# Conditional pairs for the routed blocks that may be empty, and four reorderings in the later stages of a fused kernel

## The chip, the cores and the metric

The kernel runs on one core of a Trainium2 chip. The time is the device time of one execution in microseconds (us), and the median of three runs is what counts: 2526.67 us before the change. A core has five engines that work side by side, each through its own list of instructions: TensorE (PE; its weight loads are listed as PEld), VectorE (DVE), ScalarE (ACT), GpSimd (POOL) and SyncE (SP). Data move by DMA, started from an engine's queue. All of the program is one launch.

## The reference

There are 32 sequences of 128 rows, N = 4096 rows, each with D = 512 channels. Four blocks follow each other, with a residual after the second and after the fourth:

```
# 1: shared expert plus two of eight routed experts per row
shared = (silu(x @ sw1.T) * (x @ sw3.T)) @ sw2.T
e1, e2 = top_k(sigmoid(x @ router.T + t_bias) + router_bias, 2)
out = (shared + sum_e gate_e * (gelu(x @ rw1[e].T) @ rw2[e].T)) / 3
# 2: per sequence, a policy picks one of eight weight sets
sel = argmax(policy(out[:, -1]))
x1 = x + out + 0.3 * ((gelu(out @ W1[sel] + b1[sel]) @ W2[sel] + b2[sel]) @ Wo + bo)
# 3: mix with the row before, sixteen experts by token id with a capacity
xk, xr = x1 + dx * maa_k, x1 + dx * maa_r      # dx = previous row - row
y = sigmoid(xr @ w_recept) * expert_out[slot]  # square(relu(xk @ w_key[e])) @ w_value[e]
# 4: recurrence over the 32 sequences with forget, input and candidate gates
c = sigmoid(y @ wf + c @ uf + bf) * c + sigmoid(y @ wi + c @ ui + bi) * tanh(y @ wc + c @ uc + bc)
h = tanh(y @ wo + c_final @ uo + bo); result = x1 + h
```

What each row is routed to is known only while the kernel runs.

## The kernel before

Products are made in three matmuls (`mm3`, L81): `split` (L63, L64) makes a high part on ACT (a cast to fp32r) and a low part on DVE (a subtract). Transposes are matmuls against `ident`. Tile pools hand out buffers by tag; an instruction waits until the last reader of the buffer is done. The order of instructions on each engine follows the program, but `tc.issue_after(x)` and `behind(pair)` (L71) place an instruction after x in the planned order.

The stages, with their times in the profiled execution:

- **Shared expert and router, 0 to 307 us.** The first four of eight row groups go through the shared expert. `choose` (L456) counts the rows of each expert, and pads each expert's list to blocks of 128 rows. `blk_t` holds the row numbers of a block, `blk_e` the column of its expert's weights, `end` (L496) the block at which each expert ends.
- **Routed blocks, 307 to 557 us.** At worst 71 blocks are needed (`NBLK`, 64 full ones and 7 for padding), and all 71 are always run by the loop at L689. In iteration i PE does `r_up(i)` (L658: a register load of blk_e on PE, twelve matmuls 128x256 into pur), `turn_x(i + 1)` (L283: four transposes into ptx, and a split), then `r_down(i - 1)` (L681: six matmuls 128x512 into por, a copy on DVE, a 256 KB store on SP) and `turn_h(i)` (L672: two transposes into pth, and a split). `take(i + 3)` (L275) gathers rows by an indirect DMA on POOL's queue. Blocks past the last used one hold only padding.
- **Shared expert again, 557 to 842 us.** The other four groups, with the routed rows added. In the last group `hook2` (L939) fetches the first three weight sets of the next stage and splits them with `split_w` (L878) at its chunks c = 5, 6 and 7; each split releases the gather of the weight set three further on (`fetch_w`, L859, three raw buffers).
- **Stage B, 842 to 1457 us.** A loop over the sequences (L1177) interleaves `up`, `bend` (transposes, gelu, split), `down`, each in halves a and b. `turn_r` (L1069) transposes ps and adds the bias in eight operations, four on ACT and four on DVE, into rT. Every two sequences `close` (L1086) makes x1 and xk, `mix_r` (L1134) makes xr, `send_k` (L1148, tile ptB) stores rows of xk, and `send_v` (L1158, tile pv) those of v. The weight split of a sequence is skipped when the policy picked the same set as for the one before: a branch on ACT and DVE (L891). `used` calls `split_w` after each use of a weight half.
- **Stage D, 1457 to 1834 us.** The sixteen experts. Their rows are gathered from `xk_d` once the stores of the last two `send_k` are done (rowsD, tile ptD).
- **Stage F, 1834 us to the end.** The recurrence. Its weights wc, wi and wf are fetched on ACT's queue from L1533 and uf on SP's (L1528), through a pool `stage` that is opened and closed there; rows y are gathered on POOL's queue (`get_y`, L1406) and gated (`gate_y`, L1423, tile ptF).

```
            for i in range(NBLK + 1):
                if i < NBLK:
                    r_up(i)
                    turn_x(i + 1, bx, "xb")
                    take(i + 3)
                if i > 0:
                    stored = r_down(i - 1)
                if i < NBLK:
                    turn_h(i)
```

Of the kernel before, what the change touches and what calls it, by code (L numbers as in the profile page):

```python
# [8 lines left out]
F32 = mybir.dt.float32  # L9
# [28 lines left out]
NBLK = (2 * N + E0 * (P - 1)) // P  # L38
EPS = 1e-9
# [9 lines left out]
def tile_kernel(ctx: ExitStack, tc: tile.TileContext, a: dict, out: bass.AP):  # L49
# [86 lines left out]
    blk_e = const.tile([P, NBLK], I32, name="blk_e")  # L136
    hl = const.tile([P, KD, NB], F32, name="hl")
# [10 lines left out]
    pad = const.tile([P, 448 // 4], F32, name="pad")  # L148
# [7 lines left out]
    with ExitStack() as sa:  # L156
# [117 lines left out]
        with ExitStack() as s0:  # L274
            def take(i):  # L275
                if i < NBLK:
                    xg[i] = xgp.tile([P, D], F32, tag="xg", name=f"xg_{i}")
# [5 lines left out]
            def turn_x(i, pool, tag, bufs=2):  # L283
                if i < NBLK:
# [4 lines left out]
                    if tag == "act":  # L289
# [166 lines left out]
            def choose():  # L456
# [40 lines left out]
                nc.vector.tensor_tensor(end, first, nblk, ALU.add)  # L497
                base = rtile([P, E0], "base")
# [152 lines left out]
        with s1:  # L651
# [6 lines left out]
            def r_up(i):  # L658
                with tc.issue_after(last_up[0]) if last_up else nullcontext():
                    e = nc.tensor.value_load(  # L660
                        blk_e[0:1, i : i + 1], min_val=0, max_val=(E0 - 1) * RCOL
                    )
# [9 lines left out]
            def turn_h(i):  # L672
# [4 lines left out]
                h = bx.tile([P, 2, HR // P, P], FR, tag="hb", name=f"hbr_{i}")  # L677
# [11 lines left out]
            for i in range(NBLK + 1):  # L689
                if i < NBLK:  # L690
                    r_up(i)
                    turn_x(i + 1, bx, "xb")
                    take(i + 3)
                if i > 0:
                    stored = r_down(i - 1)
                if i < NBLK:
                    turn_h(i)
                if i == NBLK - 16:
                    with tc.issue_after(stored):
                        fetch_x(NG // 2)  # L700
                if i == NBLK - 10:
# [173 lines left out]
        def bias_of(kind, b, o):  # L875
            return bcol[b][:, BIAS[kind] * KD + o : BIAS[kind] * KD + o + 1]
# [21 lines left out]
        with ExitStack() as s2:  # L898
# [40 lines left out]
            def hook2(g, c):  # L939
                sums(g, c)  # L940
                if g == last:
# [4 lines left out]
                    if c >= KF - AHEAD:  # L946
                        with behind(act_split):
                            split_w(c - KF + AHEAD)
# [15 lines left out]
    with ExitStack() as sb:  # L964
# [37 lines left out]
        def seq(p):  # L1002

            if p not in seqs:
                seqs[p] = nc.sync.value_load(seq_i[0:1, p : p + 1], min_val=0, max_val=PARTS[where(p)[0]] - 1)
            return seqs[p]

        def rows_of(t, p):

            return t[bass.ds((seq(p) + where(p)[0] * PARTS[0]) * P, P), :]  # L1010
# [58 lines left out]
        def turn_r(b):  # L1069
# [7 lines left out]
            for o in range(KD):  # L1077
                hi = rTs[c][:, 0, o, bass.ts(j, P)]
# [648 lines left out]
```

## Time and profile before

| what | value |
|---|---|
| three runs | 2520.85, 2526.67, 2529.47 us |
| profiled execution, its time | 2522.89 us |
| profiled execution, its span | 2521.2 us |
| mean granted clock of TensorE | 0.989 |
| matmuls | 13044 |
| routed blocks, 307.6 to 557.0 | 249.4 us, PE busy 247.3 |
| last matmul of the recurrence | near 2499 us |

The profile is of one execution. A page gives the busy time of each engine; the waits name, for each idle stretch of an engine, the instruction that ended it; windows give the busy times, the granted clock of TensorE and the share of the DMA engines for a stretch of time. The row of the granted clock, in 40 slices, with tenths of full speed, reads 9 almost throughout, which hides short stretches at half clock; these are seen in windows. A line number such as L660 is the kernel's, and names such as pt_0a are tiles of the program. Where several edits touch different stages, each stage is read on its own.

### The profile page before, as it was taken

What the parts mean: (1) busy time and instruction counts of PE and PEld (TensorE: products, weight loads), DVE (VectorE), ACT (ScalarE), POOL (GpSimd) and SP (SyncE); (2) the same over time, 40 slices, a digit from 0 to 9 for tenths busy, and PEclk for the clock granted to TensorE, in tenths of its full rate; (3) what the DMA queues carried; (4) which work ended last, traced back from release to release, by engine and by line L of the source; (5) the groups of instructions that cost most, each with busy time, mean ns of one, the idle gap of its engine ahead of it and who ended that gap; (6) DMA issues with size and microseconds to landing.
All of it is one profiled execution on the core that took longest, in us unless ns stands there. A gap on an engine that the chain in (4) does not pass through costs nothing. (4 is left out here: it accounts for less than half of the span.)

```text
span 2521.2 us, 37055 instructions
## 1 busy us (share of the span) xinstructions
PE 2455.6 (97%) x13044; PEld 2074.9 (82%) x13044; DVE 1331.5 (53%) x2341; ACT 1064.6 (42%) x1935; POOL 429.6 (17%) x460
## 2 busy tenths in 40 slices
PE   8999999999999899999999999999999999999996
PEld 5688899987888788888887889999978888888885
DVE  7797644556567444444454477667643323333336
ACT  4444533343223555455455466666532212222224
POOL 1000022222233333323223010000010000000003
PEclk9999999999999999999999999999999999999998
DMA  5545544457565333342342387776441111111027
GB/s 180 165 125 168 180 151 154 156 184 249 176 217 168 113 107 127 116 134 70 104 146 96 123 295 226 231 234 224 139 160 42 38 38 38 43 42 42 25 80 267
DMA packets 193117, 351.11 MB, mean 139 GB/s; under 512 B 37473, under 2 KB 72337, under 8 KB 189857
## 3 DMA queue, kind: packets, MB, share of 16 engines
q1 hardware_dynamic: 141504, 244.42, 29.6%
q0 software_dynamic: 36160, 74.90, 10.3%
q10 hardware_dynamic: 15264, 29.37, 3.2%
q8 instruction: 108, 1.77, 0.3%
q14 instruction: 81, 0.66, 0.1%
HBM read 373.94 MB, written 88.13 MB: 183 GB/s over the span
## 5 line engine op out<-in xcount | busy, mean ns | idle before, releaser
L64 DVE TENSOR_TENSOR wD<-rawD,wD 128x1024 fp32r<-128x1024 f32 x128 | 156.4, 1229 | 77.4 <-ACT wD L63 77.2
L81 PE MATMUL p<-xhl,swu 128*128 128x512 f32 x768 | 188.0, 396 | 5.5 <-ACT xhl L63 5.5
L81 PEld LDWEIGHTS phD<-xe,wD 128*128 128x128 f32 x1536 | 184.6, 189 | 1.2
L81 PE MATMUL phD<-xe,wD 128*128 128x256 f32 x1536 | 185.3, 281 | 0.0
L81 PE MATMUL p<-xhl,kept_u 128*128 128x512 f32 x768 | 184.3, 394 | 0.7 <-DVE kept_u L64 0.7
L81 PE MATMUL poD<-wD,hD 128*128 128x512 f32 x768 | 181.3, 392 | 0.0
L81 PEld LDWEIGHTS p<-xhl,swu 128*128 128x128 f32 x768 | 143.8, 189 | 36.0 <-ACT xhl L63 5.8
L81 PEld LDWEIGHTS p<-xhl,kept_u 128*128 128x128 f32 x768 | 141.8, 188 | 30.1 <-DVE kept_u L64 1.1
L81 PEld LDWEIGHTS poD<-wD,hD 128*128 128x128 f32 x768 | 142.0, 188 | 28.4
L63 ACT CAST wD<-rawD 128x1024 fp32r<-128x1024 f32 x128 | 133.1, 1046 | 53.4 <-PE poD L81 48.7
L278 POOL DMA_INDIRECT xg<-in_x_rows_dram,blk_t x71 | 67.6, 952 | 463.4 <-PE ptx L288 257.8
L1409 POOL DMA_INDIRECT y<-res_d,gat_i x32 | 33.3, 1040 | 573.9 <-DVE r L1428 495.2
L81 PE MATMUL pur<-r,xb 128*128 x852 | 118.2, 288 | 0.7 <-DVE xb L64 0.4
L81 PE MATMUL por<-r,hbr 128*128 x426 | 116.3, 407 | 1.4 <-ACT hbr L63 1.3
L64 DVE TENSOR_TENSOR xb<-ptx,xb 128x512 fp32r<-128x512 f32 x71 | 49.1, 692 | 115.3 <-ACT xb L63 115.3
L81 PEld LDWEIGHTS pur<-r,xb 128*128 128x128 f32 x852 | 105.2, 189 | 1.7 <-ACT xb L63 0.7
L81 PE MATMUL ps_f<-wf_hl,z 128*128 128x512 f32 x384 | 96.5, 399 | 0.0
L81 PE MATMUL poF<-z,wo_hl 128*128 128x512 f32 x384 | 96.4, 399 | 0.0
L81 PE MATMUL acc<-swd,as 128*128 128x512 f32 x384 | 96.0, 395 | 0.0
L81 PE MATMUL ps_c<-wc_hl,z 128*128 128x512 f32 x384 | 95.1, 395 | 0.7 <-ACT z L63 0.7
L81 PE MATMUL pb<-rT,Wo_hl 128*128 128x256 f32 x768 | 94.6, 281 | 0.0
L81 PE MATMUL pv<-w_recept_hl,xr 128*128 128x512 f32 x384 | 94.3, 395 | 0.0
(1014 smaller groups left out, 5038.3 us busy)
## 6 DMA issues: line engine op xcount, KB each, us to landing
rawD<-in_w_key_dram SPq DMA_DIRECT2D x64, 512.0 KB, 4.1
rawD<-in_w_value_dram SPq DMA_DIRECT2D x64, 512.0 KB, 3.8
swr<-in_sw_dram SPq DMA_DIRECT2D x120, 256.0 KB, 3.7
o_d<-obr SPq DMA_DIRECT2D x71, 256.0 KB, 2.4
xraw<-in_x_dram SPq DMA_DIRECT2D x32, 256.0 KB, 3.8
rraw<-in_rw_dram SPq DMA_DIRECT2D x32, 256.0 KB, 3.4
xc<-in_x_dram SPq DMA_DIRECT2D x32, 256.0 KB, 3.5
hid_d<-o ACTq DMA_DIRECT2D x32, 256.0 KB, 2.2
```

The lines of the kernel that those rows point to most:

```text
L63: first = nc.scalar.copy(hi, src).ins
L64: done = nc.vector.tensor_tensor(lo, src, hi.bitcast(F32), ALU.subtract).ins
L81: done = nc.tensor.matmul(ps, lhsT=left(hl, k), rhs=right(hr, k), start=start and k + n == 0, stop=stop and 3 * k + n == last,)
L278: nc.gpsimd.indirect_dma_start(out=xg[i], out_offset=None, in_=a["x_rows"], in_offset=bass.IndirectOffsetOnAxis(ap=blk_t[:, i : i + 1], ax ...
L1409: nc.gpsimd.indirect_dma_start(out=y, out_offset=None, in_=res_d, in_offset=bass.IndirectOffsetOnAxis(ap=gat_i[:, b : b + 1], axis=0),)
```

## The change

It has a part in each of the later stages.

1. **Routed blocks.** Blocks 0 to 63 stay unconditional. Blocks 64 to 70 form the pairs (64,65), (66,67), (68,69) and (70). Each pair runs in a conditional (`maybe`) on PE, ACT, DVE and SP that compares `used_i`, the count of blocks in use, with the pair's first block. The four conditionals stand at iterations 16, 22, 28 and 34 of the loop. The body of a pair also transposes the rows of the next pair; those of the first pair are transposed in iterations 10 and 11. The gathers of all pairs run whether or not they are used, in iterations 6, 12, 18 and 24, and each gathered tile is also stored to its block's rows of `o_d` on SP's queue; a block that runs overwrites them. On the way that is not taken, each engine waits for its own earlier instructions and then raises its semaphores.
2. **Last shared group.** The three `split_w` calls move from chunks 5, 6, 7 to 4, 5, 6.
3. **Stage B.** `turn_r` becomes one addition of the bias on DVE, written back into ps, and one split. `send_v` of a pair moves to the next iteration, one of the two between `up(a)` and `turn_r` and the other after `down(a)`. `mix_r` moves from the end of `close` to the next iteration, behind the last split.
4. **End of stage B.** The last two `send_k` store on ACT's queue, with a register load on ACT, and what follows is ordered after the store's DMA.
5. **Start of stage F.** The weights are staged in the pool `zop`, which is opened first. wc, uf and wi are fetched on SP's queue before the first gates, wf on POOL's after the first gathers of y. Products with wc and wi come before that with wf, wo is fetched after the first two tiles of y are split, and three later loads wait for a later step.

The core of the diff:

```diff
+NFULL = 2 * N // P
...
-                    xg[i] = xgp.tile([P, D], F32, tag="xg", name=f"xg_{i}")
+                    pool, tag = (xgp, "xg") if i < NFULL else (bx, "xgm")
+                    xg[i] = pool.tile([P, D], F32, tag=tag, name=f"xg_{i}")
...
+                nc.vector.tensor_copy(used_i, end[:, E0 - 1 :])
...
-            def r_up(i):
-                with tc.issue_after(last_up[0]) if last_up else nullcontext():
-                    e = nc.tensor.value_load(
-                        blk_e[0:1, i : i + 1], min_val=0, max_val=(E0 - 1) * RCOL
-                    )
+            def first_col(i):
+                return nc.tensor.value_load(blk_e[0:1, i : i + 1], min_val=0, max_val=(E0 - 1) * RCOL)
+            def r_up(i, e=None):
+                if e is None:
+                    with tc.issue_after(last_up[0]) if last_up else nullcontext():
+                        e = first_col(i)
...
+            pairs = [range(i, min(i + 2, NBLK)) for i in range(NFULL, NBLK, 2)] + [range(0)]
+            FIRST, STEP = 16, 6
+            def maybe(n):
+                es = [first_col(i) for i in pairs[n]]
+                with tc.If(used > pairs[n][0]):
+                    for i, e in zip(pairs[n], es):
+                        r_up(i, e)
+                    for m in range(2):
+                        for i in pairs[n][m : m + 1]:
+                            turn_h(i)
+                        for i in pairs[n + 1][m : m + 1]:
+                            turn_x(i, xh, "x", KD)
+                    for i in pairs[n]:
+                        r_down(i)
+                last_up.clear()
+            for i in range(NFULL + 1):
+                if i < NFULL:
                     r_up(i)
-                    turn_x(i + 1, bx, "xb")
-                    take(i + 3)
+                    if i + 1 < NFULL:
+                        turn_x(i + 1, bx, "xb")
+                    if i + 3 < NFULL:
+                        take(i + 3)
                 if i > 0:
                     stored = r_down(i - 1)
-                if i < NBLK:
+                if i < NFULL:
                     turn_h(i)
-                if i == NBLK - 16:
+                n, step = divmod(i - FIRST, STEP)
+                if i == FIRST - 4:
+                    engines = (nc.tensor, nc.scalar, nc.vector, nc.sync)
+                    used = nc.values_load(
+                        used_i[0:1, 0:1], engines=[x.engine for x in engines], min_val=NFULL, max_val=NBLK
+                    )
+                if FIRST - 6 <= i < FIRST - 4:
+                    turn_x(pairs[0][i - FIRST + 6], xh, "x", KD)
+                m, ahead = divmod(i - FIRST + STEP + 4, STEP)
+                if ahead == 0 and 0 <= m < len(pairs):
+                    for q in pairs[m]:
+                        take(q)
+                        nc.sync.dma_start(out=o_d[q * P : (q + 1) * P, :], in_=xg[q])
+                if step == 0 and 0 <= n < len(pairs) - 1:
+                    maybe(n)
...
-                    if c >= KF - AHEAD:
+                    if 4 <= c < 4 + AHEAD:
                         with behind(act_split):
-                            split_w(c - KF + AHEAD)
+                            split_w(c - 4)
...
-            for o in range(KD):
-                hi = rTs[c][:, 0, o, bass.ts(j, P)]
-                done_a = nc.scalar.activation(hi, pt[:, o, :], AF.Identity, bias=bias_of("W2a", b, o))
-                done_v = nc.vector.scalar_tensor_tensor(
-                    rTs[c][:, 1, o, bass.ts(j, P)], pt[:, o, :], bias_of("W2a", b, o),
-                    hi.bitcast(F32), ALU.add, ALU.subtract,
-                )
-            return done_a.ins, done_v.ins
+            rT = ps.rearrange("p (k q) -> p k q", k=KD)
+            bias = bias_of("W2a", b, 0, KD).unsqueeze(2).to_broadcast([P, KD, P])
+            nc.vector.tensor_tensor(rT, pt, bias, ALU.add)
+            s = bass.ts(j, P)
+            split(rTs[c][:, 0, :, s], rTs[c][:, 1, :, s], rT)
+            return tuple(last_split)
...
-            done = nc.scalar.copy(rows, pt.rearrange("p k q -> p (k q)"))
-            nc.sync.dma_start(out=rows_of(xk_d, b), in_=rows)
-            return done.ins
+            nc.scalar.copy(rows, pt.rearrange("p k q -> p (k q)"))
+            return queue.dma_start(out=rows_of(xk_d, b, queue), in_=rows).ins
...
+            gated = b - 4 if b % 2 == 0 and 0 <= b - 4 < NB - 6 else None
+            if gated is not None:
+                send_v(gated)
             if 0 <= b - 1 < NB:
                 r_done = turn_r(b - 1)
             if 0 <= b < NB:
                 down(b, "a")
                 used()
+            if gated is not None:
+                send_v(gated + 1)
...
+            if j == 0 and 0 < c < NB // PB:
+                with behind(last_split) if b + 1 < NB else nullcontext():
+                    mix_r(c - 1, end_p if c == NB // PB - 1 else bp, "xr")
...
-            if pair is not None and pair < NB - 6:
-                send_v(pair)
             if b + 1 < NB:
                 bend(b + 1, "b")
-            if pair is not None and pair < NB - 6:
-                send_v(pair + 1)
...
-                if c < NB // PB - 2:
-                    mix_r(c, bp, "xr")
-                elif c == NB // PB - 2:
-                    mix_r(c, end_p, "xr")
...
-            rows_done = send_k(b)
+            rows_done = send_k(b, nc.scalar)
...
+        zop = sf.enter_context(tc.tile_pool(name="zop", bufs=4, side="right", **kw))
...
-        with tc.tile_pool(name="stage", bufs=4, side="right", **kw) as stage:
-            uc["f"] = weight("uf", uf_p, stage, 4)
-            for b in range(LEAD):
-                nc.scalar.activation(ys[b][1], ys[b][1], AF.Sigmoid)
-            for n in "cif":
-                from_c(0, n, ps, cT, True, False)
-            wx["c"] = weight("wc", wx_p, stage, 4, queue=nc.scalar)
-            with tc.issue_after(first_part["wc"]):
-                gate_y(0)
-                gate_y(1)
-            for b in range(LEAD):
-                get_y(b + LEAD)
-            for n in "if":
-                wx[n] = weight("w" + n, wx_p, stage, 4, queue=nc.scalar)
-        zop = sf.enter_context(tc.tile_pool(name="zop", bufs=1, **kw))
+        wx_hl = {n: wx_p.tile([P, 2, KD * D], FR, tag="w" + n, name=f"w{n}_hl") for n in "ifc"}
+        wx["c"] = weight("wc", wx_p, zop, 4, pair=wx_hl["c"])
+        uc["f"] = weight("uf", uf_p, zop, 4)
+        wx["i"] = weight("wi", wx_p, zop, 4, pair=wx_hl["i"])
+        for b in range(LEAD):
+            nc.scalar.activation(ys[b][1], ys[b][1], AF.Sigmoid)
+        for n in "cif":
+            from_c(0, n, ps, cT, True, False)
+        gate_y(0)
+        z_done = gate_y(1)
+        with tc.issue_after(first_got):
+            wx["f"] = weight("wf", wx_p, zop, 4, pair=wx_hl["f"], queue=nc.gpsimd)
+        for b in range(LEAD):
+            get_y(b + LEAD)
...
-                from_x(0, ps, "cif", False, True)
-                wo1 = weight("wo", keep_p, yp, 2, "zo", KD)
+                done = from_x(0, ps, "ci", False, True)
+                with tc.issue_after(done):
+                    from_x(0, ps, "f", False, True)
+                with tc.issue_after(z_done):
+                    wo1 = weight("wo", keep_p, yp, 2, "zo", KD)
...
-                load_part(first_p, "c0", "x", 3, 0)
-                load_part(first_p, "cT0", "x", 3, 1, 2)
+                with tc.issue_after(late):
+                    load_part(first_p, "c0", "x", 3, 0)
+                    load_part(first_p, "cT0", "x", 3, 1, 2)
```

## The prediction

> **What bounds the kernel now.** I read the page's busy shares first, then TensorE's (PE's) waits, then busy time and clock stage by stage.
>
> ```profile
> PE 2455.6 (97%) x13044; PEld 2074.9 (82%) x13044; DVE 1331.5 (53%) x2341; ACT 1064.6 (42%) x1935; POOL 429.6 (17%) x460
> ```
>
> ```profile
> 307.60:557.00 249.40, 247.31 (x1701) 223.57 (x1700) 124.15 (x215) 98.79 (x221) 63.28 (x67) 1.00 0.49 161
> 842.00:1457.50 615.50, 597.36 (x3208) 504.74 (x3208) 283.45 (x543) 315.21 (x701) 180.43 (x178) 0.98 0.36 115
> ...
> 1834.20:1870.00 35.80, 31.45 (x132) 24.57 (x131) 20.76 (x26) 18.50 (x25) 10.43 (x9) 0.90 0.69 227
> ```
>
> PE is busy 97% of the span: only fewer matmuls, fewer PE gaps or a higher clock can shorten it. The rows are stretches: start and end, length, then PE, PEld, DVE, ACT and POOL busy, granted clock, DMA share. The routed blocks (first row) have almost no gap; stage B (second) loses 18 us to gaps and some to the clock; the start of the recurrence (third) is the worst in proportion.
>
> ```profile
> PE pt_0a L1050 <- ACT ue_0a L1043: 7.0, 1, 7.0
> ...
> PE ptD L1304 <- DMA rowsD<-xk_d,slot_t: 3.9, 3, 1.7
> ...
> PE ptF L1433 <- DVE z L64: 2.9, 1, 2.9
> PE pt_6a L1050 <- ACT o L756: 2.6, 1, 2.6
> PE ptB L1152 <- ACT hf_26a L1053: 2.5, 1, 2.5
> PE pt_15a L1050 <- DVEq L891: 2.1, 1, 2.1
> PE ptB L1152 <- ACT hf_16a L1053: 2.0, 1, 2.0
> ```
>
> ```profile
> 842.30:852.60 10.30, 5.42 (x15) 4.46 (x16) 3.63 (x4) 6.74 (x11) 3.81 (x3) 0.50 0.83 309
> 941.30:944.80 3.50, 3.35 (x10) 2.87 (x11) 2.41 (x8) 2.29 (x9) 2.48 (x3) 0.51 0.27 83
> ```
>
> The waits (total, times, longest) name what came last; the two windows show what a wait brings along: after several stalls of about 2 us or more the clock is granted at half for one or more steps of 3.4 us. There are six such stretches before the tail, 34.5 us in all; each 3.4 us costs up to 1.7 us.
>
> **Part 1: conditional blocks.** 71 blocks run now. The reference's own inputs give the eight experts 2559, 708, 128, 0, 373, 317, 2547 and 1560 rows, so 20+6+1+0+3+3+20+13 = 66 blocks hold rows: pair (64,65) runs, the other five blocks are skipped.
>
> ```profile
> 324.53 0.38 PE L676 MATMUL pth<-ident,ge 128*128 128x128 f32 x2
> 324.67 1.66 PE L81 MATMUL pur<-r,xb 128*128 x12
> 326.17 0.60 PE L288 MATMUL ptx<-ident,xg 128*128 128x128 f32 x4
> 326.52 1.63 PE L81 MATMUL por<-r,hbr 128*128 x6
> 327.99 0.38 PE L676 MATMUL pth<-ident,ge 128*128 128x128 f32 x2
> 328.13 1.07 PE L81 MATMUL pur<-r,xb 128*128 x7
> ```
>
> From pur to pur is 328.13 − 324.67 = 3.46 us, all PE's, so five blocks save 5 × 3.46 = 17.3 us. Against that:
>
> ```profile
> L660 PEldq TENSOR_LOAD <-blk_e x71: 297/307/492, 305.2 to 550.5; - x71
> L660 PEldq FUSED_REGOPS  x71: 151/151/165, 305.8 to 550.9; - x71
> ```
>
> A block's index reaches PE's registers through its sequencer: 0.31 + 0.15 us, and by the trace of the sequencer 0.69 us (0.68 to 0.91) until its next operation. One load per block hides, since the sequencer is some 1.25 us ahead. In the changed program's order, seven more loads stand in a row before the first branch, three more before the second, none before the others. First branch: 7 × 0.69 + 0.4 (branch, restart) − 1.25 (lead) + 0.2 = 4.2 us of idle PE. A gap this long can bring a half-clock step: 0 to 3.4, I take 1.7. Second: 3 × 0.69 + 0.4 − 1.25 + 0.2 = 1.4, and 0.5 for the skip itself; third 1.1 (on the skipped path each engine waits for its own earlier work and then signals, so PE waits for ACT's cast after pth); fourth 0.5. The body that runs turns x for 66 and 67 in vain, 8 × 0.109 = 0.9, and is pipelined less, 0.4. Sum: 4.2 + 1.7 + 1.9 + 1.1 + 0.5 + 0.9 + 0.4 = 10.7. Net −17.3 + 10.7 = **−6.6**. The seven gathers on POOL's queue and seven extra 256 KB stores on SP's lie beside PE work at a DMA share of 0.49: nothing. Without that cover a 256 KB store is worth about 2 us (the store at 1451.22 in part 4).
>
> The trace has no skip over a long body. Its nearest row is the skip of a weight split in stage B: on ACT and DVE the branch takes 45 and 56 ns, and ACT's next operation starts 0.6 us after the branch, but only four instructions are skipped. [...] Ends: −11 (no half clock, loads overlapped) to 0.
>
> **Part 2: stage B starts earlier.** The last shared group splits the first three gathered weights one chunk earlier.
>
> ```profile
> 837.37 0.62 ACT L63 CAST hidhl<-hidB 128x512 fp32r<-128x512 f32 x1 [0.42 <-ACT shc L954]
> 845.38 1.04 ACT L63 CAST wB_W2b<-rawB 128x1024 fp32r<-128x1024 f32 x1 [7.39 <-DMA rawB<-in_W2b_dram,idxw]
> ```
>
> ACT stands 7.4 us before a cast of W2b, and ue_0a, for which pt_0a waits, is behind it. The gather of W2b is released by the first split; it is issued at 835.70 and lands at 845.35. A chunk is 8.16 us, so it goes out near 827.5, when the DMA engines are idle (share under 0.03 from 820 to 836), and lands some 6 us later (the first of the three gathers took 6.4), before 837. The earlier raws landed by 807.3, so the splits moved forward at about 808, 815 and 823 don't wait. This takes the 7.0 us wait and most of the 10.3 us half-clock window (2.7 us lost in it beyond the gap): −9.7, I take **−9.5**. What is late next is hb_0a, 1 us at most.
>
> **Part 3: turn_r, send_v, mix_r.**
>
> ```profile
> L1079 ACT ACTIVATE rT<-pr,b 128x128 fp32r<-128x128 f32 x128 | 47.3, 369 | 35.3 <-DVE rT L1080 28.9 <-PE pr L1074 5.0
> ...
> L63 ACT CAST xr<-dx 128x1024 fp32r<-128x1024 f32 x16 | 16.8, 1048 | 28.6 <-DVE dx L1138 28.3
> ```
>
> Per sequence, four ACT activations and four DVE operations alternate on one PSUM tile, each waiting for the other: 4 × 0.787 = 3.15 us, with ACT idle 28.9 us in all before it. The new form is one DVE add (0.69, as a 128x512 xb row), one cast (0.63, as hidhl), one subtract (0.69): 2.0 us, with ACT work 32 × (4 × 0.369 − 0.63) = 27 us less, and DVE the same (4 × 0.355 against 2 × 0.69). The stalls of B beyond its start sum to 15 us by the spacing of matmuls, plus three half-clock steps, 4.8: 19.8 us. Most of the named ones are ACT's or DVE's being late for hf, o or a split (pt_6a, pt_15a, ptB); the shorter chain, send_v between up and down rather than after it, and mix_r's 28 us of ACT waits moved behind the split address each of them. I take two thirds, **−13.5**; ends −4 and −19.5. Every send_v pair now comes an iteration later, and its xr has about 2.1 us to spare by the trace's order; rival 3 is what happens if not.
>
> **Part 4: end of B.** The last rows are copied at 1446.2 and 1446.7, but SP, held by waits, issues their stores at 1448.36 and 1451.22; the second lands at 1453.28, and the gathers for the next stage follow at 1454.08. On ACT's queue they go out right after the copies (with one register load, 0.5 us, on ACT), so the gathers move 3.8 us forward. Stalls (4.6) and half clock (2.2) at the start of the next stage are 6.8; about 1.2 stays: **−5.5**, ends −2 and −6.8.
>
> **Part 5: start of the recurrence.** wc is issued only at 1835.68, behind ACT's copies, wi at 1840.15 and wf at 1849.2; afterwards wc, uf and wi go on SP's queue early (no release by a closed pool) and wf on POOL's. The y gathers (landing 1841.9 and 1845.5) set ptF_1 then. PE would be at the next group near 1863 to 1865 rather than 1868.3: **−4.5**, ends 0 (DMA share is 0.99 in part of this stretch, so transfers may only trade places) and −5.3.
>
> **Sum.** −6.6 − 9.5 − 13.5 − 5.5 − 4.5 = −39.6. The profiled execution took 2522.89 us (span 2521.2): 2483.3. It lies 3.8 below the median of the runs, 2526.67, so I predict **2487 us**.
>
> **Rivals.** (1) Stalls in B change place: what is freed on ACT arrives at the next wait (W splits behind gathers, xr behind dx), and only half of part 2 and 3 is kept: −11.5 rather than −23, 2498.5. For it: pt_15a waits for a split that stays; against: the largest wait has a cause that is removed. (2) The conditionals cost what they save: [...]a full half-clock step at each of two branches (+5.1 over the 1.7 taken); also if rounding in the router puts a 67th block in use, pair (66,67) runs too and +6.9 less 1.9 comes back. Part 1 is then 0, time 2493.5. (3) Slower: mix_r, now behind hidhl and the weight split on ACT, makes xr late for the first pv of each gated pair. There are 14 pairs; [...](2.5 + 1.7) × 14 = 59, time 2487 + 59 = 2546. It decides from xr ending some 5 us later than now (2.1 of slack, and 14 × 2.9 = 40 used up). Against: ACT is busy half the time in B (315 of 615 us) and gets 27 us back. (4) Parts 4 and 5 give nothing, because the same DMA engines are full there: 2497.
>
> **Chances.** Forecast 0.45, rival 1 0.23, rival 2 0.17, rival 4 0.10, rival 3 0.03; 0.02 for no change in sum. The range takes the ends of the parts: best −11 − 9.7 − 19.5 − 6.8 − 5.3 = −52.3, 2474, less the 5.8 by which the lowest run lies under the median: 2468. Worst: rivals 1 and 2 together, −21.5, and half of 4, +5, is 2510, and 3 for the highest run: 2513. About 0.3% (7.6 us) is what a measurement of this kernel can tell from no change; faster 0.95, same 0.02, slower 0.03.
>
> **What would show it.** Right: 792 pur, 396 por and 272 ptx matmuls; near 366 us a PE gap of about 4 us and three smaller ones six blocks apart; no pt_0a wait, and full clock at 842 to 852; ptB and pt_6a gone from the waits; ptD's wait under 1.5 us in all; wc's transfer on SP's queue ahead of ACT's last copies. Wrong: PE gaps of several us at every branch; xr or rT as the releaser of pv or ptB; matmul counts of 71 blocks.

## The result and the profile after

The changed kernel takes 2497.57 us (median of 6 runs, 2491.63 to 2506.37) where the kernel before takes 2524.09 us (median of 6, the three runs shown ahead and three more, 2520.78 to 2529.47): a ratio of 0.9896, 95% interval 0.9873 to 0.9918. That is 26.5 us less; 39.6 were forecast. The time lies inside the stated range, with two thirds of the gain. The profiled execution has a span of 2495.5 us, 25.7 under the one before, so the two traces can be set against each other stage by stage.

The changed kernel's page, first part, in its order of engines:

```profile
PE 2434.5 (98%) x12932; PEld 2060.7 (83%) x12932; DVE 1326.8 (53%) x2265; ACT 1034.5 (41%) x1826; POOL 412.3 (17%) x462
```

PE is busy 21 us less and idle 4.6 us less. Five blocks are not run: there are 792 pur and 396 por matmuls, 12 and 6 for each of 66 blocks, and 272 ptx, 4 for each of 68. By the forecast's 3.46 us for a block that is 17.3 of the 21 us; a matmul at half clock also counts as busy for longer (24 of pur took 5.13 us, as shown under "loads apart", where twelve take 1.66 us at full clock), and the mean granted clock rose from 0.989 to 0.991. What PE now waits for (total, times, longest):

```profile
PE po L82 <- DVE hb_0a L65: 6.7, 1, 6.7
...
PE pur L82 <- issue: 4.2, 1, 4.2
PE ptD L1348 <- DMA rowsD<-xk_d,slot_t: 2.4, 2, 1.4
PE ptF L1481 <- DVE r L1476: 2.3, 1, 2.3
PE phD L82 <- DVE hf L1367: 2.0, 1, 2.0
PE pur L82 <- PEq L702: 1.9, 1, 1.9
```

The waits of pt_0a, pt_15a and the long ones of ptB and pt_6a are gone. But po waits 6.7 us for hb_0a, about as long as pt_0a did for ue_0a, and a wait of phD for hf (2.0) is new. The two waits of pur are in the routed blocks: the first is the row of register loads ahead of the first conditional, the second a skip with four loads in a row ahead of it. The windows of the changed kernel, for the routed blocks, the start of stage B, a stretch in it, the rest of stage B, the start of stage D and that of stage F (columns as in the prediction, the last one GB/s):

```profile
305.40:548.30 242.90, 233.98 (x1589) 210.55 (x1588) 116.83 (x202) 93.16 (x208) 63.29 (x67) 0.99 0.50 167
827.60:891.40 63.80, 57.14 (x289) 47.65 (x288) 24.99 (x38) 32.12 (x68) 22.04 (x21) 0.95 0.37 115
841.40:848.30 6.90, 4.30 (x10) 3.36 (x11) 3.40 (x5) 0.00 (x0) 2.99 (x3) 0.51 0.28 78
891.40:1419.60 528.20, 525.81 (x2891) 448.45 (x2890) 258.27 (x442) 255.88 (x533) 144.97 (x156) 1.00 0.37 118
1419.60:1452.50 32.90, 28.38 (x163) 25.02 (x162) 17.26 (x19) 19.51 (x28) 8.98 (x8) 0.90 0.80 276
1809.70:1877.00 67.30, 64.33 (x285) 52.52 (x284) 30.19 (x41) 22.91 (x34) 10.98 (x13) 0.95 0.35 114
```

The rest of stage B is now at full clock with 2.4 us of idle PE in 528. The start of stage B still has 6.7 us of idle PE and 6.9 us at half clock, of which PE is busy for 4.3.

Cut at the same matmuls in both traces (the first pur, the last por, the first pu, the first and last ptB, the first and last poD, the first poF), the stretches are, in us from start to start:

| kernel | to first pur | routed blocks | first pu to first ptB | first to last ptB | to first poD | last poD to first poF |
|---|---|---|---|---|---|---|
| before | 307.6 | 249.2 | 66.6 | 543.1 | 31.1 | 68.9 |
| changed | 305.4 | 242.8 | 63.9 | 528.2 | 32.9 | 67.3 |
| all blocks | 307.8 | 248.3 | 62.3 | 528.2 | 31.5 | 68.9 |
| loads apart | 308.4 | 240.7 | 64.1 | 528.3 | 29.6 | 66.7 |
| splits at 5, 6, 7 | 305.6 | 242.1 | 62.5 | 528.1 | 31.4 | 67.5 |
| whole sum later | 310.0 | 245.4 | 55.0 | 532.3 | 32.4 | 68.7 |
| old turn_r | 306.5 | 245.1 | 65.0 | 541.4 | 30.3 | 67.3 |
| old send_v | 309.8 | 242.4 | 63.2 | 533.7 | 30.8 | 67.1 |
| stores on SP | 310.0 | 245.7 | 64.3 | 528.2 | 32.0 | 66.0 |
| old start of F | 311.9 | 243.1 | 63.5 | 528.3 | 30.8 | 70.5 |
| wi late | 309.2 | 245.2 | 61.8 | 528.3 | 30.0 | 74.2 |
| apart and sum | 312.6 | 237.8 | 55.0 | 528.3 | 31.9 | 66.5 |
| the same, splits at 5, 6, 7 | 309.3 | 239.5 | 63.3 | 528.2 | 31.7 | 67.5 |
| the same as apart and sum, wo on POOL | 308.9 | 238.9 | 55.0 | 528.2 | 31.5 | 71.5 |

The other rows are the experiments below. The first column is work that no experiment changes, and it lies between 305.4 and 312.6: that is where most of the scatter of the times comes from. The main stretch of stage B, from the first ptB to the last, repeats to 0.2 us in the ten kernels that leave it as changed. A stretch therefore tells a few microseconds apart that the time of a whole run, with an interval of some 7 us between two kernels, can't. The other stretches scatter more with the same code: the routed blocks of the changed kernel stand in eight kernels of the table and take 242.1 to 245.7 us, and the start of stage B as changed takes 61.8 to 65.0 in eight.

From before to changed: −2.2 (no change there, scatter), −6.4, −2.7, −14.9, +1.8, −1.6 in the six columns; the stretches left out, the shared groups and the steady parts of D and F, move by 0.2 us or less. The forecast had −6.6, −9.5, −13.5, −5.5, −4.5.

### The profile page after: what moved, and what is told of

It reads as the page before. It is cut to its first block, busy times and chain, and to the rows that moved or that the text cites. A ratio compares the mean times of both kernels' runs of the same rounds, so it can differ in the third digit from the quotient of the medians.

```text
span 2495.5 us, 36566 instructions
## 1 busy us (share of the span) xinstructions
PE 2434.5 (98%) x12932; PEld 2060.7 (83%) x12932; DVE 1326.8 (53%) x2265; ACT 1034.5 (41%) x1826; POOL 412.3 (17%) x462
## 4 chain that ended last, share of the span: by engine, by line
PE 49%; DVE 2%; DMA 1%; ACT 0%; issue 0%; POOL 0%; SPq 0%; POOLq 0%; DVEq 0%; ACTq 0%
PE phD L82 7%; PE ps_c L82 7%; PE ps_f L82 7%; PE ps_i L82 7%; PE poD L82 7%; PE poF L82 3%; PE po L82 3%; PE pb L82 2%; PE pv L82 1%; PE ptF L1481 1%; PE ptC L1488 1%; PE ptD L1348 0%; DMA v_d<-r 0%; DMA rawD<-in_w_value_dram 0%; PE ptB L1196 0%
## 5 line engine op out<-in xcount | busy, mean ns | idle before, releaser
L1456 POOL DMA_INDIRECT y<-res_d,gat_i x32 | 30.8, 962 | 573.6 <-DVE r L1476 492.1
L82 PE MATMUL pur<-r,xb 128*128 x792 | 111.5, 291 | 7.2 <-issue 4.2
L82 PE MATMUL por<-r,hbr 128*128 x396 | 108.0, 407 | 1.2 <-ACT hbr L64 1.2
L82 PEld LDWEIGHTS pur<-r,xb 128*128 128x128 f32 x792 | 99.7, 192 | 9.0 <-issue 6.9
```

What stands on the lines that cost most here:

```text
L82: done = nc.tensor.matmul(ps, lhsT=left(hl, k), rhs=right(hr, k), start=start and k + n == 0, stop=stop and 3 * k + n == last,)
L1456: got = nc.gpsimd.indirect_dma_start(out=y, out_offset=None, in_=res_d, in_offset=bass.IndirectOffsetOnAxis(ap=gat_i[:, b : b + 1], axis=0),)
```

## The experiments

My theory from the two traces: parts 1 and 3 work as forecast; part 2 removes its wait but another, behind a DMA, ends at nearly the same time; parts 4 and 5 mostly trade one transfer against another. Each experiment starts from the changed kernel unless it says otherwise. Ratios are to the kernel before, which ran on the same chip; the changed kernel's is 0.9896.

**All blocks.** The edits of part 1 are undone.

```diff
-            for i in range(NFULL + 1):
+            for i in range(NBLK + 1):
...
-                if step == 0 and 0 <= n < len(pairs) - 1:
-                    maybe(n)
```

> The changed kernel with its first part undone: all 71 blocks run, no conditionals, nothing else differs. By the two traces the routed blocks end 6.4 us earlier relative to their start, so this kernel should be 6 us slower than the changed one: a ratio to before near 0.992 where the changed kernel had 0.9896, and a blocks stage of 249 us with no half-clock step at 367. Rival: the conditionals cost what they save in the median too, and the ratio stays at 0.990.

2507.56 us, ratio 0.9924 (0.9909 to 0.9939). The routed blocks take 248.3 us, 5.5 more, and no half-clock step follows near 367. By these two kernels the conditionals are worth 5.5 us in the stretch and 7 in the time. The changed kernel is one of the quicker of its eight, though: their middle is 244.1, by which the conditionals are worth 4.2 us against this run and 5.1 against the kernel before.

**Loads apart.** The register loads move.

```diff
             def maybe(n):
-                es = [first_col(i) for i in pairs[n]]
+                with tc.issue_after(last_up[0]):
+                    e_next[:] = [first_col(FIRST + STEP * n + 1)]
                 with tc.If(used > pairs[n][0]):
-                    for i, e in zip(pairs[n], es):
-                        r_up(i, e)
+                    for i in pairs[n]:
+                        r_up(i, first_col(i))
...
-                    r_up(i)
+                    r_up(i, e_next.pop() if e_next else None)
```

> The changed kernel, but the registers of a conditional pair are loaded inside the conditional, and the load for the next ordinary block is placed ahead of the branch at its usual distance. Ahead of the first branch only the load of the count of used blocks is left in a row with the ordinary one. If the row of eight loads makes the 4.2 us wait of pur and the 6.8 us of half clock after it (3.4 lost), both go: the first branch costs about 1 us, the body about 1 us for its first load, and the time is 5 to 7 us under the changed kernel's (ratio to before 0.987). Rival: the wait is the branch itself[...]; then a gap of 3 us or more and the half clock stay, and the time with them.

2494.9 us, ratio 0.9871 (0.9854 to 0.9887). PE's timeline at the first conditional, first in the changed kernel and then in this one (start, length, engine, line, operation, tiles, count, and in brackets the idle time before it):

```profile
364.65 0.38 PE L682 MATMUL pth<-ident,ge 128*128 128x128 f32 x2
369.27 5.13 PE L82 MATMUL pur<-r,xb 128*128 x24 [4.23 <-issue]
...
401.25 1.82 PE L82 MATMUL pur<-r,xb 128*128 x12 [1.91 <-PEq L702]
```

```profile
368.48 1.78 PE L82 MATMUL pur<-r,xb 128*128 x12 [0.56 <-issue]
370.79 1.75 PE L82 MATMUL pur<-r,xb 128*128 x12 [0.53 <-issue]
...
397.99 1.79 PE L82 MATMUL pur<-r,xb 128*128 x12 [0.51 <-ACTq L704]
```

In the changed kernel PE stands 4.23 us, and then 24 matmuls of pur take 5.13 us, at half clock; with the loads apart two gaps of 0.5 us remain, at full clock. So the wait is the row of eight loads (seven of block columns and the one of the count), not the branch, which took 0.09 us in the changed kernel and still stands there with the loads apart. The second conditional, which is skipped (the third row and the last), shows the same: 1.91 us with four loads in a row ahead of it, 0.51 without. The stretch is only 2.2 us shorter here: between 496 and 505 us there is 1.1 us more of gaps than in the kernel "apart and sum", and a half-clock step at 501.9. That kernel has the same loads and no such step, and its stretch is 5.1 us shorter. In all four kernels with the loads apart it takes 237.8 to 240.7 us, with a middle of 239.2, 4.9 under the middle of the eight with the rows of loads.

**Splits at chunks 5, 6, 7.** Part 2 undone.

```diff
-                    if 4 <= c < 4 + AHEAD:
+                    if c >= KF - AHEAD:
                         with behind(act_split):
-                            split_w(c - 4)
+                            split_w(c - KF + AHEAD)
```

> The changed kernel with the second part undone: the three splits of gathered weights are back at chunks 5, 6 and 7. My prediction gave this part 9.5 us; the trace of the changed kernel shows a wait of 6.7 us for hb_0a in place of the 7.0 us for ue_0a, and about 2.7 us in all by then. By the traces this kernel is 2 to 4 us slower than the changed one (ratio near 0.991); by the prediction 9.5 us slower (0.9935).

2501.3 us, ratio 0.9897 (0.9883 to 0.9911), where the changed kernel has 0.9896. The stretch from the first pu to the first ptB is 62.5 us, within the 61.8 to 65.0 of the kernels with the part. It is worth nothing here that could be told from scatter, less than both expectations. In this kernel pt_0a waits 5.8 us for ue_0a instead.

**The whole sum later.** What hb_0a waits for is read from DVE's timeline in the changed kernel:

```profile
830.38 1.23 DVE L65 TENSOR_TENSOR wB_W2b<-rawB,wB_W2b 128x1024 fp32r<-128x1024 f32 x1 [1.92 <-ACTq L934]
841.63 0.75 DVE L793 SCALAR_TENSOR_TENSOR o<-o,g,shc 128x512 f32<-128x512 f32 x1 [10.02 <-DMA shc<-sh_d]
842.59 0.75 DVE L794 SCALAR_TENSOR_TENSOR o<-o,g,o 128x512 f32<-128x512 f32 x1 [0.21 <-DVEq L934]
843.26 0.68 DVE L65 TENSOR_TENSOR hb_0a<-hf_0a,hb_0a 128x512 fp32r<-128x512 f32 x1
```

hb_0a's subtract could have run at 835, when ACT had done its cast (834.20 to 834.82). It stands in DVE's list behind the sum for sequence 28, an operation that the program needs five sequences later, and that sum waits 10 us for shc, the shared expert's part of it, to be read back from memory. The read is issued at 832.4, when the DMA engines are full (share 1.00 from 830 to 838) with the gathers, x, hidB and Wo.

```diff
-            if 0 <= late < GB and step == 2:
+            if 0 < late < GB and step == 2:
                 combine(NB - GB + late, ps_t)
...
+            if late == 0 and step == 2:
+                with behind(last_split):
+                    combine(NB - GB, ps_t)
```

> The changed kernel, but the sum for sequence 28 (L793, which reads shc back from memory) is ordered behind the split of hb_6a rather than being free to run first in stage B. If DVE stands in that sum until the DMA of shc lands and hb_0a's subtract is merely queued behind it, the 6.7 us wait of po and the half clock after it (3.4 lost) go, and the kernel is 7 to 10 us faster than the changed one (ratio near 0.986). Rival: the start of stage B is bound by what its DMA engines have to bring (share 1.00 from 830 to 838), so another transfer, hidB or W1a, is late next and at most 3 us is won.

2496.45 us, ratio 0.9867 (0.9849 to 0.9885). The stretch falls from 63.9 to 55.0 us: the 7 to 10 expected. The rival, that the next transfer is late, is out. But PE then waits 3.6 us for the sum at 934 us, since its transposes were ordered with it, and the next stretch is 4.1 us longer: half of the gain is given back.

**Old turn_r.** Its eight operations of before, everything else as changed.

```diff
-            nc.vector.tensor_tensor(rT, pt, bias, ALU.add)
-            split(rTs[c][:, 0, :, s], rTs[c][:, 1, :, s], rT)
+            for o in range(KD):
+                hi = rTs[c][:, 0, o, bass.ts(j, P)]
+                done_a = nc.scalar.activation(hi, pt[:, o, :], AF.Identity, bias=bias_of("W2a", b, o))
+                done_v = nc.vector.scalar_tensor_tensor(
+                    rTs[c][:, 1, o, bass.ts(j, P)], pt[:, o, :], bias_of("W2a", b, o),
+                    hi.bitcast(F32), ALU.add, ALU.subtract,
+                )
```

> The changed kernel with turn_r as before (four ACT and four DVE operations that alternate), all else changed. Stage B from its first ptB to its last ptB is 14.9 us shorter in the changed kernel. If turn_r's shorter chain earns most of it, this kernel is 8 to 12 us slower than the changed one (ratio to before 0.993 to 0.994). Rival: the moved send_v and mix_r earn it, and this kernel is within 4 us of the changed one.

2515.83 us, ratio 0.9963 (0.9949 to 0.9977). Stage B takes 541.4 us, 13.2 more, which is above the 8 to 12 expected, and PE's waits show the alternating chain:

```profile
PE ptB L1198 <- DVE rT L1126: 7.1, 7, 3.4
...
PE pt_6a L1095 <- DVE rT L1126: 2.3, 1, 2.3
```

**Old send_v.** Their places of before, and mix_r's.

```diff
-            if gated is not None:
-                send_v(gated)
...
-            if j == 0 and 0 < c < NB // PB:
-                with behind(last_split) if b + 1 < NB else nullcontext():
-                    mix_r(c - 1, end_p if c == NB // PB - 1 else bp, "xr")
...
+            if pair is not None and pair < NB - 6:
+                send_v(pair)
...
+                if c < NB // PB - 2:
+                    mix_r(c, bp, "xr")
```

> The changed kernel with send_v and mix_r at their places of before, all else changed. If turn_r earns most of stage B's 14.9 us, this one is 3 to 6 us slower than the changed kernel (ratio 0.991 to 0.992); by the rival 10 us or more (0.994).

2507.38 us, ratio 0.9927 (0.9913 to 0.994). Stage B takes 533.7 us, 5.5 more, within the 3 to 6 expected. So against before's 543.1 the new turn_r alone saves 9.4 us, the new order alone 1.7, and both 14.9, 3.8 more than their sum: neither expectation had it that each is worth more with the other. With the old order PE still waits for the branch of a weight split on DVE:

```profile
PE pt_6a L1095 <- DVEq L934: 2.2, 1, 2.2
...
PE ptB L1196 <- DVEq L934: 2.1, 1, 2.1
```

**Stores on SP.** Part 4's queue undone.

```diff
-            rows_done = send_k(b, nc.scalar)
+            rows_done = send_k(b)
```

> The changed kernel with the last two stores of xk on SP's queue, as before. My prediction gave the move to ACT's queue 5.5 us. In the changed kernel's trace the second store is issued at 1423.2, just after the first has landed at 1423.1, so the queue is not what it waits for: by the trace this kernel is 0 to 2 us slower (ratio 0.990), by the prediction 5.5 us (0.992).

2501.81 us, ratio 0.9901 (0.9887 to 0.9916). From the last ptB to the first poD it takes 32.0 us, where the kernels with the stores on ACT's queue take 29.6 to 32.9: nothing is won that this stretch shows. In the trace of the changed kernel the first store is issued at 1420.19, lands at 1423.08, and the second is issued at 1423.21. The second waits for the first on SP's queue too, as the chain of the kernel before shows (start, length; the stores are issued at 1448.36 and 1451.22):

```profile
1448.36 2.75 DMA xk_d<-rows
...
1451.22 2.06 DMA xk_d<-rows
```

What ACT's queue does win is the start of the first store: the gathers behind both come 7.1 us after the last ptB in the changed kernel and 9.0 here. But then PE waits elsewhere. In the changed kernel phD waits 2.0 us for hf (rows of DVE and of PE):

```profile
1446.14 1.22 DVE L65 TENSOR_TENSOR wD<-rawD,wD 128x1024 fp32r<-128x1024 f32 x1 [0.69 <-ACT wD L64]
1447.28 0.68 DVE L1367 TENSOR_TENSOR hf<-rl,phD 128x512 f32<-128x512 f32 x1
...
1448.10 4.60 PE L82 MATMUL phD<-xe,wD 128*128 128x256 f32 x24 [1.98 <-DVE hf L1367]
```

Here, and in the kernel before, phD has no such wait. That the earlier gathers bring it on is read from these traces, not tested.

**Apart and sum.** The loads apart, and the sum's two DVE operations as a step of its own (`add_rows`), behind the split of hb_4a and ahead of its transposes, which stay where they were.

```diff
+            if b == 3:
+                with behind(last_split):
+                    add_rows(NB - GB)
```

> The changed kernel with the register loads of the conditionals placed as in the run with loads inside the conditionals, and the two DVE operations of sequence 28's sum held behind the split of hb_4a, its transposes left where they were. The earlier run that held back the whole sum took the 6.7 us wait and its half clock away (8.9 us gone between the first pu and the first ptB) but had PE wait 3.6 us for that sum later. If both effects add up and that later wait is avoided, the time is 13 to 16 us under the changed kernel's (ratio 0.983 to 0.9845). Rival: the freed DMA time moves the wait to W's gathers or hidB, and only the 6 us of the loads remain (0.987).

2486.71 us, ratio 0.9838 (0.9825 to 0.9851): the fastest kernel of the study, 40 us under before. The window of its start of stage B, and DVE there:

```profile
830.20:885.20 55.00, 55.00 (x290) 46.38 (x289) 23.64 (x36) 32.21 (x68) 21.98 (x21) 1.00 0.40 129
```

```profile
833.03 1.23 DVE L65 TENSOR_TENSOR wB_W2b<-rawB,wB_W2b 128x1024 fp32r<-128x1024 f32 x1 [1.92 <-ACTq L941]
837.50 0.69 DVE L65 TENSOR_TENSOR hb_0a<-hf_0a,hb_0a 128x512 fp32r<-128x512 f32 x1 [3.25 <-ACT hb_0a L64]
```

PE is busy in all of the 55 us at full clock; hb_0a waits for its own cast and for nothing else.

**The same with the splits at 5, 6, 7.** Part 2 undone in the fastest kernel, with the diff of the third experiment.

> The fastest kernel so far (loads of the conditionals apart, sum of sequence 28 held back, ratio 0.9838) with the three weight splits back at chunks 5, 6 and 7. There the stretch from the first pu to the first ptB took 55.0 us. If the second part was worth its 9.5 us all along and was only hidden by the sum's wait for shc, this kernel has the wait of pt_0a for ue_0a again, 61 to 64 us for the stretch and a ratio of 0.9865 to 0.9875. Rival: without the sum the gather of W2b lands in time anyway, and nothing changes (0.984).

2496.29 us, ratio 0.9875 (0.986 to 0.989) against 0.9838: 9.4 us slower. The wait of before is back:

```profile
PE pt_0a L1102 <- ACT ue_0a L1095: 6.2, 1, 6.2
```

The stretch is 63.3 us rather than 55.0. With the sum out of its way part 2 is worth about its forecast.

**Old start of F.** Part 5 undone.

```diff
-        wx["c"] = weight("wc", wx_p, zop, 4, pair=wx_hl["c"])
-        uc["f"] = weight("uf", uf_p, zop, 4)
-        wx["i"] = weight("wi", wx_p, zop, 4, pair=wx_hl["i"])
...
+        with tc.tile_pool(name="stage", bufs=4, side="right", **kw) as stage:
+            uc["f"] = weight("uf", uf_p, stage, 4)
...
+            wx["c"] = weight("wc", wx_p, stage, 4, queue=nc.scalar)
```

> The changed kernel with the fifth part undone (start of stage F as before). My prediction gave this part 4.5 us. From the last poD to the first poF the traces have 68.9 us before and 66.0 to 68.9 us in the kernels with the part, so I expect 1 to 3 us more time (ratio 0.990 to 0.9908), with 68 to 69 us for this stretch. By the prediction: 4.5 us more (0.9914).

2505.23 us, ratio 0.9911 (0.9896 to 0.9926). From the last poD to the first poF it takes 70.5 us, more than the 68 to 69 expected; before took 68.9, and the ten kernels with the part as it is took 66.0 to 68.9. Against the middle of those, 67.3, it is worth 1.6 to 3.2 us; the times alone would allow the forecast 4.5.

**wi late.** wi moves from SP's queue to POOL's behind the first gathers of y.

```diff
-        wx["i"] = weight("wi", wx_p, zop, 4, pair=wx_hl["i"])
...
         with tc.issue_after(first_got):
+            wx["i"] = weight("wi", wx_p, zop, 4, pair=wx_hl["i"], queue=nc.gpsimd)
```

> The changed kernel, but wi too is fetched on POOL's queue behind the first gathers of y, so that 1 MB less is in flight when the last rows of stage D are stored. If the early weight loads are what delays the store of res and with it the gathers of y (the second res store issued at 1810.7, the gather only at 1816.3, where before it was 1835.0 and 1837.8), the gather comes within 3 us of the store, ptF's wait of 2.3 us shrinks and the stretch from the last poD to the first poF is 1 to 3 us shorter, unless wi is then late itself. Rival: the gathers wait for something else and nothing changes.

2508.25 us, ratio 0.9924 (0.9911 to 0.9938), slower. The issues of the last store of res and the first gather of y, in the changed kernel and then here:

```profile
1810.73 0.33 ACTq L1384 DMA_DIRECT2D res_d<-ob  x1
1816.25 0.95 POOL L1456 DMA_INDIRECT y<-res_d,gat_i  x1 [80.87 <-DMA res_d<-ob]
```

```profile
1812.39 0.33 ACTq L1384 DMA_DIRECT2D res_d<-ob  x1
1815.38 1.14 POOL L1456 DMA_INDIRECT y<-res_d,gat_i  x1 [78.34 <-DVE wc_hl L65]
```

The gather does come 3.0 us after the store rather than 5.5, and it is no longer the store that releases it: early loads do hold that store up. But wi and wf are then fetched late, and PE waits for wf:

```profile
PE ps_f L82 <- ACT wf_hl L64: 5.7, 1, 5.7
```

**wo on POOL.** The fastest kernel with wo's loads behind four gathers of y on POOL's queue.

```diff
-            get_y(b + LEAD)
+            next_got = get_y(b + LEAD)
...
-                with tc.issue_after(z_done):
-                    wo1 = weight("wo", keep_p, yp, 2, "zo", KD)
+                with tc.issue_after(next_got):
+                    wo1 = weight("wo", keep_p, yp, 2, "zo", KD, queue=nc.gpsimd)
```

> The fastest kernel so far (ratio 0.9838) with wo fetched on POOL's queue behind the first four gathers of y, so that 0.5 MB less is in flight when the last rows of stage D are stored, and wi stays early. If the early loads delay that store, the gathers of y come 1 to 2 us earlier, the stretch from the last poD to the first poF falls from 66.5 to about 65 us, and the ratio is 0.983. Rival: wo is then late for its splits, or the later gathers of y wait behind it, and the stretch is longer (67 us or more, ratio 0.9845).

2493.95 us, ratio 0.9866 (0.9847 to 0.9884), slower, as the rival had it; the stretch is 71.5 us. ptC waits 6.3 us for the first new c. ACT's timeline shows why:

```profile
1824.40 0.63 ACT L1485 ACTIVATE r<-r 128x512 f32<-128x512 f32 x1 [5.51 <-DMA r<-v_d]
1824.93 0.61 ACT L1519 ACTIVATE v_c<-v_c 128x512 f32<-128x512 f32 x1
```

The gates' tanh stands behind a sigmoid whose r is late, as its load (issued 1811.74, landed 1824.04) now shares the DMA engines with wf, wo and the bias rows: 12.3 us, where the same load of the fastest kernel took 6.2 (1817.16 to 1823.35). Neither shift of a load helped: in both runs what was taken from one transfer was paid at another.

## Why the prediction was right or wrong

**Part 1 was right in its mechanism; that its sum fits so well is partly luck.** The row of eight loads gave a PE gap of 4.2 us, as worked out from the 0.69 us of one; the second conditional 1.9, as worked out, and the skip alone, with the loads apart, 0.51 for the 0.5 taken. The term for the half clock, 1.7, was half of its largest value, a guess. Here 6.8 us were granted at half, from 367.0 on, but PE's gap lasted until 369.27, so 2.3 of them passed in idleness. The 24 matmuls of pur then took 5.13 us where some 3.2 would do at full clock (an estimate from the 1.66 us of twelve): about 2 us lost, for 1.7. The third and fourth conditionals cost less than their 1.1 and 0.5: 0.3 us on the third, none named on the fourth. The stretch came to −6.4 against −6.6 with this trace, but the middle of the eight kernels is 4.2 to 5.1 us under the two with all blocks. Four of the eight have a second, separate half-clock step and lie at 245.1 to 245.7: three of them near 405, behind the gap of 1.9 us at the second conditional, which brings none in the other five. That much of rival 2, a step at each of two branches, did come. A skip itself is short: with the loads apart the three skips over PE's long body leave gaps of 0.51, 0.45 and 0.30 us.

**Part 2 was wrong in its place, right in its size.** The failed step is "What is late next is hb_0a, 1 us at most". I took hb_0a's time from the engine work ahead of it. What stood ahead of it on DVE was the sum for sequence 28, with a DMA behind it; the trace of before shows it too, 2.06 us of DVE hidden behind the longer wait for W2b:

```profile
851.39 0.81 DVE L750 SCALAR_TENSOR_TENSOR o<-o,g,shc 128x512 f32<-128x512 f32 x1 [2.06 <-DMA shc<-sh_d]
```

Moving the split earlier left that read where the full DMA engines put it: with a DMA share of 1.00 from 830 to 838 it was issued at 832.4 and DVE had its data only at 841.63. Only 2.7 us came by the two traces, and none by the run without the part. Rival 1 named this in general (half of parts 2 and 3 kept), but put its place at W's splits and xr. With the sum moved away the part gives 9.4 us by the times and 8.4 by the stretch, against 9.5.

**Part 3 was right**: −14.9 for −13.5. The two thirds of 19.8 were a guess; the mechanism is what the runs bear out. The chain of turn_r was the larger part (9.4 us alone), and the new order pays little without it (1.7). Rival 3 did not come: the longest wait of pv is 0.4 us. Its price, 2.5 us of stall and 1.7 of half clock for each of 14 pairs, was an estimate: in the trace of before the clock stays at 1.00 behind the 2.13 us that PE waits for pt_15a (at 1113.63) and the 3.01 us for rt (at 17.99). ACT's wait before xr went from 28.6 us to 4.8.

**Part 4 was wrong** at "the gathers move 3.8 us forward", and at what waits next. Counted from the last ptB the gathers come at 7.1 us instead of 8.4, 1.3 earlier, since the second store waits until the first has landed, whichever queue it is on (issued 0.13 us after the landing on ACT's, 0.11 on SP's). What the 1.3 us brought is lost again at phD, which waits 2.0 us for hf: hf could have run at 1444.7, when ACT's part of it was done, but DVE has it behind the subtract of a wD whose raw weights landed only at 1444.3 and were then cast. The stretch came to +1.8 for −5.5. I had priced the queue and not the order of two stores to one tensor.

**Part 5 was half right**: −1.6 in the traces, 1.6 to 3.2 by the experiment, against 4.5. The low end that I named, transfers trading places, is what happens: y's gathers no longer share the DMA engines with wc (whose cast starts at 1810.6), but they wait for the store of res, which shares them with the early wi, r and wo: those are issued from 1803.5 to 1806.4, the DMA share is 0.98 from 1808 to 1812, and the gather comes 5.5 us after the store.

**Sum.** 39.6 were forecast. By the two traces part 2 fell short by 6.8 us, part 4 by 7.3 and part 5 by 2.9, part 3 gave 1.4 more, and the parts together 23.8; 2.2 us of the difference between the traces are the scatter of the first stretch. Of the signs named ahead, the matmul counts and the gaps of the conditionals came; full clock at 842 to 852 did not (half clock from 841.4 to 848.3), nor a wait of ptD under 1.5 us (2.4). Rival 1's 2498.5 is near the measured time, but for a reason that is only partly its own. What is left open: how long the second store of xk has to wait for the first was read, not varied; and when a gap brings a step of half clock: the one at 501.9 has no long wait ahead of it, and the same gaps bring a step in one kernel and none in the next. In the trace of before there is also one step more than the six I counted, 3.4 us from 30.0 on, behind a wait of 1.9 us.

## What to carry to other kernels

When a wait is to be removed, list what stands behind it on every engine of the next consumer, in the order of issue and not in the order of need, and ask each one's DMA when it lands; a shorter wait hidden under the long one is already in the trace of before. An operation that is ready early by the plan but reads memory back belongs behind the operations that the next matmul needs: here the sum held DVE for 10.0 us. Put register loads of a conditional inside it or spread them at the usual distance: here the row of eight cost 4.2 us of idle PE, and by my estimate about 2 us more at half clock.

## What the runs showed that I had not expected

The row of eight loads cost 4.2 us of idle PE, and the half clock behind it about 2 us more by my estimate. With the loads apart, and again with the old turn_r, a half-clock step came at 501.9 and 503.9 with no long gap ahead of it, after four of 0.34 to 0.89 us within 5 us, at a late block of the routed experts. Four such gaps (0.84, 0.59, 0.59 and 0.33 us) in the fastest kernel with the splits at 5, 6, 7 brought none. On PE the branch itself took 93 to 362 ns (median 216, five branches), where ACT took 45, SP 48 and DVE 56.
